# One decoder block on one core: the last two pairs' routing by straight logits, places written at once, and later deviations

## The chip, the cores and the metric

The kernel runs on one core of one Trainium2 chip. The metric is device time in microseconds, the median of three runs. One further execution was recorded by the hardware profiler; its trace gives the rows quoted here. Engines: PE is TensorE's matmul side (PEld its loading of weights), DVE VectorE, ACT ScalarE, POOL GpSimd, SP SyncE, which issues most of the DMAs. L1563 is line 1563 of the kernel before.

## The reference

One decoder layer over 16 sequences of 256 tokens of width 256, with a layer norm behind each of three residual parts. In the first attention the scores are `s / s`; the kernel forms that as a product of two such ratios, one of the queries and one of the keys, and weighs the values with its exps. The second is a differential cross attention: two softmaxes over the context, the second subtracted with a gain, each head then normalized. The third is a mixture of four experts with the two best chosen for each token:

```python
logits = jnp.einsum('bsh,he->bse', x, router_w) + router_b + load_balancer
rw, sel = jax.lax.top_k(logits, K)
rw = jax.nn.softmax(rw, axis=-1)
...
gathered = jnp.take_along_axis(stack, sel[..., None], axis=2)
return (rw[..., None] * gathered).sum(axis=2)
```

The change touches the end of the cross attention and the routing.

## The kernel before

**Tiles.** Two sequences make a pair (512 tokens, four chunks of 128); there are eight pairs, 0 to 7. The activations stay in SBUF in `xs`, tokens on partitions. Each expert gets only the tokens that chose it. For that every token's row is written by an indirect DMA, a "put" (L453), into a list in DRAM, at a place computed on the chip; there are two lists, one for pairs 0 to 6 and one for pair 7. A chunk has two puts, one for each chosen expert, so a pair has eight.

**Steps.** The cross attention runs as numbered steps. A step is a quarter of a unit (a pair, one of its sequences, four heads): score matmuls (`p`), the maximum on DVE, and three units later the scores again with exps on ACT (`e`), then the weighing `pob`. Other work is hung onto the steps by a small planner: `plan.at` and `later` run a function in a given step, `ahead` puts it first in its step, `job` queues it from a first step on with a due step. PE, DVE and ACT keep the order in which the code emits their instructions; POOL's and SP's orders in this stretch are chosen by the framework's scheduler from the dependences.

**The chain at the end of a pair.** `finish1` turns the weighed values back (pn, L1476), divides and subtracts (o on DVE, ob and the squares osq on POOL, L1485 and L1486). `finish2` makes the deviations of the heads: a sum on DVE (hv, L1493), then on POOL a reciprocal root by Newton steps and a product (L1494 to L1497). `finish4` turns the result (pto, L1506), `finish5` multiplies (pf) and adds (L1519), `norm` normalizes rows (POOL, up to L205). When both sequences are through, `turn_tokens` (pty, L1537) and the logits follow: `logits` holds the router's weights stationary, four chunks beside each other in 32 columns each; ACT copies the result (L1558), `turn_logits` turns it back on PE (ptl, L1563) and adds the bias on DVE. `routing` is a generator of five stages on DVE, POOL and ACT (selection, exp at L411, weights at L435). `places` counts with matmuls (pl), copies the lengths on DVE (L1581), and hands over to `listing`: rows (L442), then for each chunk the places on DVE (L451) and two puts. When a group's last pair is listed, POOL casts the counts (L463), waiting for all puts.

**The start of the experts.** `begin` loads the second expert's first two blocks of 512 rows from the list, every engine reads five counts (`known`, L500), and the first block is turned (pt, L527). The second expert's blocks (`early`) are mixed with the rest of pair 7: each is a turn of a later block, 16 matmul passes pw, 32 passes pr, and a store by SP (L556). Pair 7's finish, logits, routing and puts fall between these blocks.

`roomy(q)` is true for pairs 0 to 5. For pairs 6 and 7 nothing is spread over spare steps.

Of the kernel before, what the change touches and what calls it, by code (L numbers as in the profile page):

```python
# [15 lines left out]
P = 128  # L16
# [4 lines left out]
NPAIR = B // 2  # L21
TB = 2 * S
CPB = TB // P
# [77 lines left out]
def bc(ap, axis, n):  # L101

    shape = list(ap.shape)
    return ap.unsqueeze(axis).to_broadcast(shape[:axis] + [n] + shape[axis:])
# [3 lines left out]
def decoder_kernel(ctx: ExitStack, tc: tile.TileContext, a: dict, out: bass.AP):  # L108
# [46 lines left out]
    def mm(out_, lhsT, rhs, start=True, stop=True):  # L155
        PE.matmul(out=out_, lhsT=lhsT, rhs=rhs, start=start, stop=stop)  # L156
# [193 lines left out]
    moe, puts = {}, ([], [])  # L350

    def group(q):
        return int(q >= GROUPS[1][0])
# [35 lines left out]
    def routing(q, lg):  # L389

        ra = moe[q] = {}

        def tt(name, shape=(P, CPB, 4)):
            if name in ("gt", "eq", "sel", "mx"):
                return tiny.tile(list(shape), F32, tag=name, name=name)
            return moe["pool"].tile(list(shape), F32, tag=name, name=name, bufs=2 if name == "accs" else 1)

        gt, eq = tt("gt", (P, CPB, 4, 4)), tt("eq", (P, CPB, 4, 4))
        DVE.tensor_tensor(gt, bc(lg, 2, 4), bc(lg, 3, 4), ALU.is_gt)
        DVE.tensor_tensor(eq, bc(lg, 2, 4), bc(lg, 3, 4), ALU.is_equal)  # L400
        POOL.tensor_tensor(eq, eq, bc(moe["tri"], 1, CPB), ALU.mult)
        POOL.tensor_tensor(gt, gt, eq, ALU.add)
        yield
        larger, mx = tt("larger"), tt("mx", (P, CPB))
        DVE.tensor_reduce(larger, gt, AX.X, ALU.add)
        DVE.tensor_reduce(mx, lg, AX.X, ALU.max)
        sel = ra["sel"] = tt("sel")
        POOL.tensor_scalar(sel, larger, 2.0, None, ALU.is_lt)
        POOL.tensor_tensor(lg, lg, bc(mx, 2, 4), ALU.subtract)
        yield  # L410
        ACT.activation(lg, lg, AF.Exp)  # L411
        accs = ra["accs"] = tt("accs", (P, CPB + 1, 4))
        if q == GROUPS[group(q)][0]:
            POOL.memset(accs[:, 0], 0.0)
        else:
            POOL.tensor_copy(accs[:, 0], moe[q - 1]["accs"][:, CPB])
        for n in range(CPB):
            POOL.tensor_tensor(accs[:, n + 1], accs[:, n], sel[:, n], ALU.add)
        POOL.tensor_tensor(lg, lg, sel, ALU.mult)
        fore = tt("gt", (P, CPB, 4, 4))  # L420
        POOL.tensor_tensor(fore, bc(sel, 2, 4), bc(moe["tri"], 1, CPB), ALU.mult)
        yield
        den, nth = tt("mx", (P, CPB)), tt("nth")
        DVE.tensor_reduce(den, lg, AX.X, ALU.add)
        DVE.tensor_reduce(nth, fore, AX.X, ALU.add)
        DVE.reciprocal(den, den)
        both = ra["both"] = tt("both", (P, 2, CPB, 4))
        POOL.tensor_scalar(nth, nth, 1.0, None, ALU.is_lt)
        POOL.tensor_tensor(both[:, 0], sel, nth, ALU.mult)
        POOL.tensor_tensor(both[:, 1], sel, both[:, 0], ALU.subtract)  # L430
        POOL.tensor_tensor(lg, lg, bc(den, 2, 4), ALU.mult)
        w2 = tt("eq", (P, 2, CPB, 4))
        POOL.tensor_tensor(w2, both, bc(lg, 1, 2), ALU.mult)
        yield
        DVE.tensor_reduce(  # L435
            moe["weight"][:, q * CPB:(q + 1) * CPB, :].rearrange("p n k -> p k n"), w2, AX.X, ALU.add
        )
        yield
# [879 lines left out]
    def cross_attention(wb, r1, ps1):  # L1318
# [7 lines left out]
        for mp in mpads:  # L1326
# [5 lines left out]
        plan = Plan(  # L1332
            finish1=.55, turn_x=.55, turn_keys=.55, turn_tokens=.55, finish4=.55, project=1.05, values=1.9, finish5=1.9,
            logits=.6, turn_logits=.2, places=.6, weigh=1.85,
        )
# [3 lines left out]
        def apart():  # L1339
            return 1 if plan.now >= SINGLE else 2  # L1340
# [3 lines left out]
        cxs, xTs, es, ovs, oas, os_, sqs, ots = ({} for _ in range(8))  # L1344

        def bank(name):
            return banks[0].tile([P, 512], F32, tag="sm", name=name)
# [122 lines left out]
        def finish1(q, b, ic, t):  # L1470

            o = os_[q, b]
            pn = bank("pn")
            for k in range(4):
                i0 = t * S + ic * P
                PE.transpose(pn[:, k * P:(k + 1) * P], ovs[q, b, k][:, i0:i0 + P], ident)  # L1476
            pn_v = pn.rearrange("p (h d) -> p h d", h=H)
            rd = tiny.tile([P, H], F32, tag="rd", name="rdb")
            DVE.reciprocal(rd, pn_v[:, :, 16])
            if t == 1:  # L1480
                DVE.tensor_scalar(rd, rd, sec["gain"], None, ALU.mult)
            oas[t] = late[0].tile([P, H, HD], F32, tag="o2", name="o2", bufs=4)
            DVE.tensor_tensor(oas[t], pn_v[:, :, 0:16], bc(rd, 2, HD), ALU.mult)  # L1483
            if t == 1:
                POOL.tensor_tensor(o[:, ic], oas[0], oas[1], ALU.subtract)  # L1485
                POOL.tensor_tensor(sqs[q, b][:, ic], o[:, ic], o[:, ic], ALU.mult)  # L1486
                if ic == 1:
                    plan.later(4 if (q, b) <= (NPAIR - 2, 0) else 2, finish2, q, b)

        def finish2(q, b):  # L1490

# [36 lines left out]
        def roomy(q):  # L1528
            return q < NPAIR - 2

        def slack(q):
            return 3 if roomy(q) else 0
# [14 lines left out]

        def logits(q):

            pl = bank("pl")[:, :P]  # L1550
            for c in range(2):
                for n in range(CPB):
                    mm(
                        pl[32 * n:32 * n + 32, :], moe["rw"][:, c].rearrange("p a e -> p (a e)"),
                        xTs[q, c][:, n * P:(n + 1) * P], c == 0, c == 1,
                    )
            lT = moe["pool"].tile([P, P], F32, tag="lT", name="lT")
            ACT.copy(lT, pl)  # L1558
            plan.job(plan.now + apart(), plan.now + apart() + slack(q), turn_logits, q, lT)

        def turn_logits(q, lT):
            pt = bank("ptl")
            PE.transpose(pt[:, :P], lT, ident)  # L1563
            pl = pt[:, :P].rearrange("p (n a e) -> p n a e", n=CPB, e=4)[:, :, 0]
            lg = tiny.tile([P, CPB, 4], F32, tag="lg", name="lg")
            DVE.tensor_tensor(lg, pl, bc(moe["rb"], 1, CPB), ALU.add)
            route = routing(q, lg)
            for k in range(5):
                plan.ahead(1 + (2 * k if roomy(q) else k), next, route, None)
            wait = (FREE - 9 - plan.now) % 16 if roomy(q) else 0  # L1570
            plan.job(plan.now + 6 + wait, plan.now + 6 + wait + slack(q), places, q)

        def places(q):

            ra = moe[q]
            pb = bank("pl")
            pl = pb[:, :4 * CPB].rearrange("p (n e) -> p n e", e=4)
            if q + 1 == GROUPS[group(q)][1]:
                mm(pb[:, 4 * CPB:4 * CPB + 4], moe["ones"], ra["accs"][:, CPB])
                n = moe["length"]  # L1580
                DVE.tensor_copy(n[:, :4], pb[:, 4 * CPB:4 * CPB + 4])  # L1581
                DVE.tensor_tensor(n[:, 4:5], n[:, 0:1], n[:, 2:3], ALU.max)
            mm(pl, moe["before"], ra["sel"], True, False)
            mm(pl, moe["ones"], ra["accs"][:, :CPB], False, True)
            rows = moe["pool"].tile([P, CPB, 4], F32, tag="rows", name="rows")
            DVE.tensor_tensor(rows, pl, bc(moe["base"][:, group(q), :], 1, CPB), ALU.add)
            steps = listing(q, rows)
            plan.later(1, next, steps, None)
            plan.later(2, next, steps, None)
            for k in range(CPB):  # L1590
                if q < NPAIR - 3:
                    t = plan.now + 3 + (FREE - 3 - plan.now) % 16 + 4 * k
                else:
                    t = plan.now + (3 + 4 * k if q == NPAIR - 3 else 2 + k)
                plan.at(t, next, steps, None)
            plan.at(t + 1, next, steps, None)

# [151 lines left out]
```

## Time and profile before

| what | value |
| --- | --- |
| median of three runs | 1674.32 us (1673.7 to 1676.51) |
| profiled execution, device time | 1684.38 us |
| its span, first to last instruction | 1682.7 us, granted TensorE clock 0.983 |
| the cross attention's exps (L1435), first and last start | 605.7 and 1181.1 us |
| the first expert block's transposes begin | 1198.84 us |

The stretch that the change touches lies between about 1150 and 1290 us. The busy time of each engine in stages of it (from a table of windows; x is the number of instructions, then granted clock, DMA share and GB/s):

```profile
1170.00:1180.00 10.00, 8.43 (x61) 5.42 (x60) 1.40 (x10) 5.54 (x12) 6.50 (x28) 0.89 0.01 2
1180.00:1190.00 10.00, 8.37 (x44) 4.00 (x40) 3.01 (x10) 2.22 (x4) 5.85 (x7) 0.77 0.18 66
1190.00:1200.00 10.00, 1.16 (x6) 1.17 (x7) 0.00 (x0) 0.01 (x1) 3.34 (x5) 0.57 0.45 144
1200.00:1210.00 10.00, 10.00 (x36) 6.10 (x35) 3.19 (x9) 4.99 (x7) 4.08 (x16) 0.92 0.51 159
```

After the length of the window the columns are PE, PEld, DVE, ACT and POOL. PE is busy in nearly all of every window but the third, where it does 1.16 us in 10.

### The profile page before, as it was taken

The numbers are of one execution on the slowest core, as the hardware profiler recorded it, in microseconds if no ns is written. First come the engines' busy times: TensorE is split into PE (matmuls) and PEld (weight loads), VectorE is DVE, ScalarE is ACT, GpSimd is POOL, SyncE is SP. The second block draws the span as 40 slices with busy tenths as digits, with TensorE's granted clock in tenths as the row PEclk, the third lists the DMA queues.
The fourth block names the chain that finished last, engine by engine and source line by source line (L and its number), as shares of the span: only waits on it lengthen the run. The fifth ranks groups of instructions, "written<-read, shape, count | busy, mean of one in ns | idle before, by whom it ended". The sixth has DMA issues, their size and how long they took to land. (4 is left out here: it accounts for less than half of the span.)

```text
span 1682.7 us, 32337 instructions
## 1 busy us (share of the span) xinstructions
PE 1596.8 (95%) x12238; PEld 928.0 (55%) x12238; DVE 948.0 (56%) x1985; ACT 942.1 (56%) x1392; POOL 578.7 (34%) x1252
## 2 busy tenths in 40 slices
PE   7999999999999899999999999999799999899994
PEld 2333443444444466666666666665466566766673
DVE  2226656566666787777777777775213242323447
ACT  3557777888787856666666666666233211233212
POOL 5001243132123441243545535376331101046533
PEclk8999999999999999999999999999799999999997
DMA  9932121222222300000001000010326010132323
GB/s 251 302 106 70 64 72 64 74 67 67 98 65 76 115 15 2 16 2 15 28 20 35 15 16 21 9 40 27 102 86 220 1 51 14 54 113 64 95 65 126
DMA packets 118587, 115.34 MB, mean 69 GB/s; under 512 B 8208, under 2 KB 112352, under 8 KB 118400
## 3 DMA queue, kind: packets, MB, share of 16 engines
q1 hardware_dynamic: 109376, 93.08, 17.3%
q0 software_dynamic: 7824, 19.65, 3.8%
q8 instruction: 113, 1.85, 0.5%
q14 instruction: 74, 0.61, 0.1%
q10 hardware_dynamic: 1200, 0.15, 0.1%
HBM read 73.79 MB, written 38.54 MB: 67 GB/s over the span
## 5 line engine op out<-in xcount | busy, mean ns | idle before, releaser
L1429 DVE TENSOR_REDUCE mpad<-p 128x4 f32<-128x1024 f32 x256 | 303.3, 1217 | 114.2 <-PE p L156 109.3
L943 ACT ACTIVATE h<-ph,L_attn_b 128x1024 f32<-128x1024 f32 x256 | 271.2, 1111 | 140.8 <-PE ph L156 136.9
L1435 ACT ACTIVATE e<-p 128x512 f32<-128x512 f32 x512 | 269.7, 600 | 136.8 <-PE p L156 131.2
L156 PE MATMUL p<-qp,kT 32*128 32x256 f32 x2048 | 286.2, 393 | 4.4 <-issue 3.1
L156 PE MATMUL p<-kT,qp 32*128 32x256 f32 x2048 | 275.2, 392 | 3.9 <-DVE mpad L1429 3.8
L156 PEld LDWEIGHTS p<-kT,qp 32*128 32x128 f32 x2048 | 194.8, 184 | 50.3 <-issue 19.9
L156 PEld LDWEIGHTS p<-qp,kT 32*128 32x128 f32 x2048 | 206.9, 184 | 22.1 <-issue 8.1
L156 PE MATMUL ph<-qT,w1p 32*128 32x512 f32 x1024 | 163.7, 645 | 5.4 <-ACT h L943 4.2
L1044 DVE TENSOR_TENSOR z<-rqb,ra 128x1024 f32<-128x1024 f32 x120 | 151.5, 1268 | 3.1 <-DMA rqb<-rqd 3.1
L156 PE MATMUL pe<-h,w2p 128*32 128x512 f32 x1024 | 135.8, 600 | 0.0
L1051 ACT ACTIVATE z<-z 128x1024 f32<-128x1024 f32 x120 | 126.6, 1057 | 0.3 <-DVE z L1044 0.3
L156 PE MATMUL pob<-e,vaug 128*32 128x512 f32 x1024 | 124.6, 605 | 0.1
L156 PEld LDWEIGHTS ph<-qT,w1p 32*128 32x128 f32 x1024 | 47.6, 184 | 123.9 <-ACT h L943 88.6
L201 POOL TENSOR_SCALAR ln_ve<-ln_mv 128x2 f32<-128x2 f32 x32 | 8.8, 276 | 247.9 <-DVE ln_mv L199 246.8
L205 POOL TENSOR_SCALAR xs<-xs,ln_mv,rs_y 128x256 f32<-128x256 f32 x64 | 85.5, 1341 | 2.8
L156 PE MATMUL pw<-xeT,L_ffn_sw_w 128*128 128x512 f32 (+1 forms) x256 | 83.3, 486 | 1.9 <-PEq L734 1.9
L156 PE MATMUL po<-z,vaug 128*32 128x256 f32 x1024 | 73.2, 385 | 5.7 <-ACT z L1051 3.6
L453 POOL DMA_INDIRECT xlist<-xs,place x64 | 64.0, 1000 | 35.2 <-DVE place L451 13.2
L156 PEld LDWEIGHTS pw<-xeT,L_ffn_sw_w 128*128 128x128 f32 x256 | 48.6, 190 | 35.3 <-issue 31.0
L1485 POOL TENSOR_TENSOR ob<-o,o 128x256 f32<-128x256 f32 x32 | 23.5, 735 | 124.4 <-DVE o L1483 111.9
L156 PE MATMUL pw<-xeT,L_ffn_ml_w 128*128 128x512 f32 (+1 forms) x160 | 63.3, 552 | 0.3 <-DVE ye L555 0.3
L528 ACT ACT_TABLE_LOAD x16 | 20.5, 1283 | 76.6 <-PE pt L527 76.3
(378 smaller groups left out, 2582.2 us busy)
## 6 DMA issues: line engine op xcount, KB each, us to landing
rqb<-rqd SPq DMA_DIRECT2D x64, 512.0 KB
xlist<-zero SPq DMA_DIRECT2D x16, 1024.0 KB
xe<-xlist SPq DMA_DIRECT2D x20, 512.0 KB
xlist<-ye SPq DMA_DIRECT2D x14, 512.0 KB
xs<-in_x SPq DMA_DIRECT2D x8, 512.0 KB
cx<-in_ctx SPq DMA_DIRECT2D x8, 512.0 KB
qp<-st SPq DMA_DIRECT2D x256, 2.0 KB
out<-xs SPq DMA_DIRECT2D x7, 512.0 KB
```

Of the source, the lines that this page charges most:

```text
L156: PE.matmul(out=out_, lhsT=lhsT, rhs=rhs, start=start, stop=stop)
L201: POOL.tensor_scalar(ve, mv[:, :, 1], EPS, None, ALU.add)
L205: POOL.tensor_scalar(x, x, mv[:, i, 0:1], r[:, i:i + 1], ALU.subtract, ALU.mult)
L453: put = POOL.indirect_dma_start(xlist[g][:], bass.IndirectOffsetOnAxis(ap=place[:, n, k:k + 1], axis=0), xs[:, q * CPB + n, :], None)
L528: copies[c](t[:, c, :n * P], pt[:, :n * P])
L943: ACT.activation(h, phs[gp], AF.Tanh, bias=b1[:, fc:fc + 1])
L1044: DVE.tensor_tensor(z, bc(rqbs[u][:, 2 * gp:2 * gp + 2], 2, 2), bc(rk, 3, S), ALU.mult)
L1051: ACT.activation(z, z, AF.Exp)
L1429: DVE.tensor_reduce(mpads[j % 2][:, 2 * gp:2 * gp + 2, :, ic], p1, AX.X, ALU.max, negate=True)
L1435: ACT.activation(e[:, gi], p2[gi], AF.Exp)
L1485: POOL.tensor_tensor(o[:, ic], oas[0], oas[1], ALU.subtract)
```

## The change

Three edits, none of which changes what is computed:

1. The puts of pairs 6 and 7: all four chunks' places and puts are emitted in the same step, two steps after `places`; before, chunk k came k steps later.
2. The deviations (`finish2`) of pair 7's first sequence come eight steps after `finish1` in place of two, and those of its second sequence four in place of two. All others keep theirs.
3. The logits of pairs 6 and 7: each chunk's tokens are the stationary operand and the router's four columns the moving one, so that the result has tokens on partitions at once. The copy on ACT and the transposition on PE go, and the routing starts in the step of the logits, one step earlier. Pairs 0 to 5 keep the old way; the tail of `turn_logits` becomes the function `route`.

```diff
                 if ic == 1:
-                    plan.later(4 if (q, b) <= (NPAIR - 2, 0) else 2, finish2, q, b)
+                    plan.later({(NPAIR - 2, 1): 2, (NPAIR - 1, 0): 8}.get((q, b), 4), finish2, q, b)
...
         def logits(q):
 
+            if not roomy(q):
+                pl = bank("pl")[:, :4 * CPB].rearrange("p (n e) -> p n e", e=4)
+                for n in range(CPB):
+                    for c in range(2):
+                        mm(pl[:, n, :], xTs[q, c][:, n * P:(n + 1) * P], moe["rw"][:, c, 0], c == 0, c == 1)
+                return route(q, pl)
             pl = bank("pl")[:, :P]
...
             PE.transpose(pt[:, :P], lT, ident)
-            pl = pt[:, :P].rearrange("p (n a e) -> p n a e", n=CPB, e=4)[:, :, 0]
+            route(q, pt[:, :P].rearrange("p (n a e) -> p n a e", n=CPB, e=4)[:, :, 0])
+
+        def route(q, pl):
             lg = tiny.tile([P, CPB, 4], F32, tag="lg", name="lg")
             DVE.tensor_tensor(lg, pl, bc(moe["rb"], 1, CPB), ALU.add)
-            route = routing(q, lg)
+            stages = routing(q, lg)
             for k in range(5):
-                plan.ahead(1 + (2 * k if roomy(q) else k), next, route, None)
+                plan.ahead(1 + (2 * k if roomy(q) else k), next, stages, None)
...
-                    t = plan.now + (3 + 4 * k if q == NPAIR - 3 else 2 + k)
+                    t = plan.now + (3 + 4 * k if q == NPAIR - 3 else 2)
```

In the instruction order of the changed kernel, against the one before: PE's place matmuls of pair 6 stand two score quarters earlier; pair 7's first pto stands between the transposes of the first two expert blocks, where one pn stood, and its pf behind the first block's product; on POOL the eight puts of pair 6 stand together, behind them the chain L1494 to L1497 of pair 7's first sequence, then the cast of the counts; on SP the load of the fifth block stands behind the first store.

## The prediction

> **What bounds the kernel now.** I read the busy row and the slices first, then PE's waits between 1100 and 1320 us, where every instruction that the diff touches runs, then the timelines of PE, POOL, ACT and DVE there.
>
> ```profile
> PE 1596.8 (95%) x12238; PEld 928.0 (55%) x12238; DVE 948.0 (56%) x1985; ACT 942.1 (56%) x1392; POOL 578.7 (34%) x1252
> ```
>
> TensorE is busy almost throughout, so a change in this stretch pays only where PE stands still. Its waits there (who waited for whom: us in total, times, longest) begin with
>
> ```profile
> PE pt L527 <- DMA xe<-xlist: 9.8, 1, 9.8
> PE pt L527 <- issue: 2.5, 1, 2.5
> PE pl L156 <- DVE length L1581: 2.3, 2, 1.6
> ```
>
> One long wait: the transposes of the first expert block, for rows loaded from the list in DRAM. PE's timeline (columns: start, us, engine, line, tiles, count, idle time before) shows its ends, POOL's what it hangs on:
>
> ```profile
> 1187.19 1.89 PE L156 MATMUL pf<-L_xattn_woT,otb 128*128 128x256 f32 x8
> 1198.84 1.97 PE L527 MATMUL pt<-ident,xe 128*128 128x128 f32 x8 [9.76 <-DMA xe<-xlist]
> ```
>
> ```profile
> 1179.80 1.07 POOL L453 DMA_INDIRECT xlist<-xs,place  x1 [0.70 <-DVE place L451]
> ...
> 1187.59 0.96 POOL L453 DMA_INDIRECT xlist<-xs,place  x1 [2.92 <-DVE rdb L1479]
> ...
> 1192.52 0.99 POOL L453 DMA_INDIRECT xlist<-xs,place  x1 [0.17 <-issue]
> 1195.20 0.18 POOL L463 CAST count<-length 128x5 int32<-128x5 f32 x1 [1.69 <-DMA xlist<-xs,place]
> ```
>
> The eight puts of pair 6 (L453) complete the list. The last ends at 1193.51, the queue issues the load 1.45 us later, at 1194.96, and the rows are there 3.88 us after that. Beside it runs a second path: the cast of the counts (L463), then every engine reads five counts (L500; PE's first starts at 1195.4, the last at 1197.3 for 0.31), so PE could have gone on at 1197.6. The rows were later, by 1.2 us. Behind 1198.84 PE is dense for the 90 us in which the second expert runs, so what moves PE's restart, or adds PE work behind it, moves the end.
>
> **Part 1: when the list is complete.** Pair 6's logits begin at 1162.05 on PE. Now 8 matmuls, packed four abreast in 32 columns, take 0.57 us (next instruction 1162.62), ACT copies the result, PE transposes it at 1167.35 (0.26 to the next start). After the change each of the 8 has 128 tokens as weights and four moving columns. The before trace has no such logits; it has the same shape at the bias products (128x128 weights, one moving column, two passes a matmul):
>
> ```profile
> 113.96 0.60 PE L156 MATMUL pb<-L_ffn_me_eq_b,m 128*128 128x1 f32 x4
> 114.42 0.58 PE L156 MATMUL pb<-L_ffn_me_bv,m 128*128 128x1 f32 x4
> 114.87 0.58 PE L156 MATMUL pb<-L_ffn_me_bo,L_ffn_me_c1w 128*128 128x1 f32 x4
> ```
>
> Starts 0.455 apart for four passes: 0.112 us a pass, 16 passes 1.80 us. Here a rule is to be weighed. The Trainium skill, "TensorE: Matmul & The Clock Gate", section Back-to-back issue gap, gives a matmul of 1 to 64 moving columns about 25 ns: 16 passes would be 0.40 us (an estimate from that page). The same page's section on LDWEIGHTS says that loading goes by weight columns, 128/1.2 = 107 ns. The row says that the weights set the pace here, so I take 1.80; with 0.40 the whole sum below would be about 1.4 us better at pair 6 and 1.4 at pair 7, -3.4 in place of -0.6. From the other side, the plain transposes go at 0.148 a pass (four in 0.59): 2.4 us each time.
>
> So PE is 1.80 - 0.57 - 0.26 = 0.97 later at the score quarter that now starts at 1167.61. From there ACT's exps set the pace (they run unbroken from 1168.77 to 1171.81), and the exp of the logits (L411) slips between them for 0.11 (now 1171.64 to 1171.75). The weighing pob of 1171.94 starts at 1173.02 and takes 1.86: the places' matmuls start at 1174.88, now 1175.70, because two quarters (1.90 us) that stand ahead of them are behind them in the new order.
>
> Now they stall there: the first starts at 1175.70, the second at 1177.62, since DVE copies the lengths (L1581) only after the weights (L435), which wait for POOL's routing, which is interleaved with pair 7's deviations (L1494 to L1497, 1169.17 to 1175.46). With the deviations moved behind the puts, and the logits on DVE at 1164.1 in place of 1167.71, I follow the routing row by row to the weights at about 1173.2, before PE comes; 0.60 (0.36 and the copy) are left. Second matmul: 1175.48. From it to the first put takes 2.18 as now (1177.62 to 1179.80): 1177.66.
>
> Puts: four now wait 2.92 us for their places on DVE, behind reciprocals that wait for PE, and let ob and osq in between: 13.71 us from 1179.80 to 1193.51. With all places written at once they run as pair 7's eight do now, 1269.22 to 1279.17, 9.95 us. **Last put: 1187.6, 5.9 us earlier.**
>
> **Part 2: what is late next.** The moved deviations come back. In the instruction order of the changed kernel POOL has, between the last put and the cast, the whole chain L1494 to L1497 of pair 7. Undisturbed it takes 5.52 us (1129.90 to 1135.42). The rows land at 1187.6 + 1.45 + 3.88 = 1192.9. The cast, which could run at 1189.3, ends at 1187.6 + 0.1 + 5.52 + 0.18 = 1193.4, and PE reads five counts for 2.23 us more: **PE restarts at 1195.6**, not 1198.84, a gain of 3.2. The wait changes hands from the DMA to the counts, and 2.7 of the 5.9 stay behind.
>
> **Part 3: PE work moved over the gap.** Now PE does pair 7's first pto and pf (L1506 at 1180.49, pf at 1187.19) ahead of its wait, for nothing. In the new order the fourth pn goes ahead, the pto takes its place between the first blocks' transposes (0.59 for 0.59), and the pf stands behind the first block's product: +1.83 us (the other pf, 1232.14 to 1233.97), on the path.
>
> What waits for it: DVE's residual (L1519), the deviations of (7,1) (hv L1493 is behind it in DVE's order) and POOL's two chains, which are interleaved. hv comes about 3.4 us after the first block's end, and 7.5 us of POOL end 10.9 after it; the pto that needs them comes after 1.83 + 0.87 + 13.9 = 16.6. Cover 5.7 us, so nothing. The load of block 4 moves behind the first store on SP: needed 34 us later, nothing.
>
> **Part 4: pair 7's logits,** on the path too. Now the first half starts at 1249.95 beside ACT's second copy, and the next transposes at 1251.67. In the new order the first matmul waits for both copies, 1250.69, and 1.80 us follow: 1252.49, **+0.82**. ACT's lT copy and the transposition are in the 1251.67 already. Pair 7's places come 14 us later, behind the block's product, and its puts stand together now: nothing from that edit.
>
> **Sum:** -3.2 + 1.83 + 0.82 = -0.55. The profiled execution (span 1682.7 of 1684.38) should read about 1682.1; on the median of the runs, 1674.32, the same microseconds give **1673.7**. A second rule bears on the gap: the same page, part 1, lets PE run at half clock after an idle window of about 3.4 us, until a busy one. The granted clock was 0.60 from 1198.8 to 1202.4, and the 20 transposes there took 3.60 us against 2.33 at the warm pace: 1.27 lost, by the rule 1.7. PE's work before the gap ends near 1185, so 10 us of idle time remain and neither is won back.
>
> **Rivals.**
> - Counts in time (0.12): the cast or the reading of the counts costs less than I take, and PE restarts with the rows, at 1192.9: -5.9 + 2.65 = -3.3, 1671.0, or more if the logits are cheaper too. For it: the reading is hidden in the trace, and POOL's chain has short steps. Against it: the order is fixed, the chain stands before the cast.
> - Puts that throttle each other (0.11): two puts of pair 5 at 1162.98 and 1165.31 stood 2.33 us apart with nothing shown between, not 1.27. If four of the eight pay that 1.06, the last put ends at 1191.8, PE restarts at 1199.8, and the sum is +1.0 + 2.65 = +3.6: 1677.9. It decides from a mean spacing of about 1.8 us. Against it: pair 7's eight, back to back at 1.28.
> - Dear logits (0.07, no change in the end): 2.4 us each, +0.6 twice: +0.6, 1674.9.
> - The early places don't come early, because the routing is late for PE as now (0.05): 2.1 of the 5.9 are lost, +1.6, 1675.9.
>
> **How the numbers follow.** Forecast 0.65, 1673.7, its own range 1671.8 to 1675.6 (5.0 to 5.8 for the chain, 1.7 to 2.4 for the logits, 1 us for places on ACT's pace). A measurement of this kernel can tell about 0.2%, 3.3 us, from no change. The forecast, dear logits and late places lie within it (0.77, of which I give 0.02 to the edge): same 0.75. Faster has its rival and a little of that edge, 0.13; slower has the puts' rival and the rest, 0.12. The range that leaves 2 in 10 out is 1670.6 to 1677.4.
>
> **What would show it.** Right: the last L453 of pair 6 near 1187.6 and without waits among the eight; L463 some 5.7 us behind it, released by POOL's own chain; the first pt<-xe at 1195 to 1196, waiting for counts and no more for the DMA; a pf of 1.8 us behind the first block's pr; pl at pair 7 as 16 passes of 0.11. Wrong: puts further apart than 1.3 us, pl matmuls that stall for DVE again, or a wait of pto for POOL in the second expert's blocks.

## The result and the profile after

| kernel | median | runs |
| --- | --- | --- |
| before | 1675.74 us | 1673.7 to 1676.51, 6 runs |
| changed | 1682.4 us | 1678.56 to 1684.91, 6 runs |

The changed kernel is slower: ratio 1.0036, 95% interval 1.0023 to 1.0049, or some 6 us, where 0.6 us less was forecast. (The three runs of before given above are among the six here.) In two later comparisons it gave 1.0014 (1.0004 to 1.0025) and 1.0035 (1.0022 to 1.0048).

PE's waits in the stretch, in the same view as before (who waited for whom: us in total, times, longest):

```profile
PE pt L527 <- POOL ob L1485: 8.8, 1, 8.8
PE pt L527 <- issue: 2.5, 1, 2.5
...
PE pl L156 <- DVE length L1589: 1.0, 2, 0.8
```

The long wait has changed hands as forecast: the rows (DMA) no longer end it. The name ob is that of the last POOL instruction that the trace could tie to it; what PE waited for is the count, as POOL's timeline shows (start, us, engine, line, tiles, count, idle before):

```profile
1179.78 1.07 POOL L453 DMA_INDIRECT xlist<-xs,place  x1 [0.70 <-DVE place L451]
...
1188.74 0.96 POOL L453 DMA_INDIRECT xlist<-xs,place  x1 [0.30 <-issue]
1189.77 0.22 POOL L1494 TENSOR_SCALAR hv<-hv 128x32 f32<-128x32 f32 x1
1194.22 1.06 POOL L1497 TENSOR_TENSOR ob<-ob,rs_y 128x512 f32<-128x512 f32 x1
1195.22 0.19 POOL L463 CAST count<-length 128x5 int32<-128x5 f32 x1
```

Eight puts in 9.92 us, none waiting, then the moved chain, then the cast. But the first put is late, and PE's timeline shows why:

```profile
1159.47 1.95 PE L156 MATMUL pl<-rw,x 128*128 128x4 f32 x16
1161.34 1.13 PE L156 MATMUL p<-qp,kT 32*128 32x256 f32 x8
...
1162.99 2.09 PE L156 MATMUL p<-qp,kT 32*128 32x256 f32 x8
1165.01 3.64 PE L156 MATMUL pob<-e,vaug 128*32 128x512 f32 x16
...
1177.28 0.39 PE L156 MATMUL pl<-accs,ones 128*128 128x4 f32 x2
1177.91 0.40 PE L156 MATMUL pl<-sel,before 128*128 128x16 f32 x2 [0.26 <-DVE length L1589]
```

The logits take 1.87 us from start to start. The eight score matmuls behind them take 1.13 us, the next eight 2.09, and the weighing pob 3.64. In the profile of before the same stretch reads

```profile
1162.05 0.65 PE L156 MATMUL pl<-x,rw 128*32 128x128 f32 x16
...
1164.35 1.21 PE L156 MATMUL p<-qp,kT 32*128 32x256 f32 x8
1165.49 1.92 PE L156 MATMUL pob<-e,vaug 128*32 128x512 f32 x16
```

So PE of the changed kernel runs at about half speed from 1163 on. In windows of 2 us (length, PE, PEld, DVE, ACT, POOL, then granted clock, DMA share, GB/s):

```profile
1160.00:1162.00 2.00, 2.00 (x19) 1.93 (x20) 0.51 (x3) 0.56 (x2) 1.23 (x2) 1.00 0.04 14
1162.00:1164.00 2.00, 2.00 (x15) 1.50 (x13) 0.85 (x4) 1.08 (x2) 1.26 (x2) 0.83 0.15 51
1164.00:1166.00 2.00, 2.00 (x13) 0.69 (x14) 0.41 (x3) 1.09 (x2) 1.92 (x6) 0.50 0.18 66
1166.00:1168.00 2.00, 2.00 (x16) 0.26 (x8) 0.00 (x0) 0.00 (x0) 1.07 (x6) 0.50 0.00 0
1168.00:1170.00 2.00, 2.00 (x15) 1.35 (x15) 0.00 (x0) 0.58 (x1) 0.00 (x0) 0.50 0.00 0
```

PE counts as busy 2.00 us of every 2.00, and its clock falls to 0.50 all the same. In the profiled execution of before the clock was 1.00 up to 1177, for instance

```profile
1164.00:1166.00 2.00, 2.00 (x20) 1.20 (x22) 0.92 (x3) 1.30 (x3) 0.69 (x1) 1.00 0.18 66
```

Executions differ in when they reach this stretch (the start of pair 6's logits, t0, lay between 1159.4 and 1163.5 us), so traces are compared from t0. All marks in us behind it; "pair 7 through" is the first transposes behind pair 7's logits, "end" the transposes ahead of pr<-xw (1293.09 in the profile of before):

| kernel | first places' matmul | first put | last put ends | cast ends | PE restarts | pair 7 through | end |
| --- | --- | --- | --- | --- | --- | --- | --- |
| before, profile shown | 13.65 | 17.75 | 31.46 | 33.33 | 36.79 | 89.62 | 131.04 |
| before, second trace | 15.29 | 17.76 | 29.68 | 31.55 | 35.17 | 89.50 | 130.92 |
| forecast | 12.83 | 15.61 | 25.55 | 31.35 | 33.55 | 89.07 | |
| changed, profile | 17.81 | 20.31 | 30.23 | 35.94 | 38.16 | 93.52 | 135.02 |
| changed, second trace | 15.95 | 18.46 | 28.38 | 34.09 | 36.34 | 91.82 | 133.30 |
| changed, third trace | 16.00 | 18.50 | 28.43 | 34.14 | 36.37 | 92.58 | 135.52 |

When pair 7 is through the changed kernel is 2.2 to 4.0 us behind before, at the end of the stretch 2.3 to 4.6.

### The profile page after: what moved, and what is told of

It reads as the page before. It is cut to its first block, busy times and chain, and to the rows that moved or that the text cites. A ratio compares the mean times of both kernels' runs of the same rounds, so it can differ in the third digit from the quotient of the medians.

```text
span 1676.9 us, 32328 instructions
## 1 busy us (share of the span) xinstructions
PE 1596.9 (95%) x12236; PEld 927.8 (55%) x12236; DVE 945.5 (56%) x1985; ACT 941.4 (56%) x1390; POOL 579.7 (35%) x1252
## 3 DMA queue, kind: packets, MB, share of 16 engines
q8 instruction: 112, 1.84, 0.4%
## 5 line engine op out<-in xcount | busy, mean ns | idle before, releaser
L156 PE MATMUL pob<-e,vaug 128*32 128x512 f32 x1024 | 129.6, 626 | 0.1
L1462 ACT COPY ovTb<-pob 128x512 f32<-128x512 f32 x64 | 37.5, 585 | 61.7 <-PE pob L156 61.7
```

The source lines that it names most:

```text
L1462: ACT.copy(o, po)
```

## The experiments

Kernels of one group ran on the same chip, beside the kernel before.

**First group: the parts alone.** Theory: the straight logits bring PE's clock down and eat the gain. Rival: the moved work (POOL's chain ahead of the counts, pf behind the gap) costs more than reckoned.

*before_again* is the kernel before, unedited.

> The kernel before, unchanged, for a second trace of it. Expected ratio 1.000. In the trace: 36.8 us from the start of pair 6's logits to the first transposes of the first expert block (xe), and a granted clock of 1.00 in the 10 us after those logits. If the half clock seen there in the changed kernel is chance and not its logits, it may show up here too.

Measured: 0.9998 (0.9989 to 1.0007). The clock is 1.00 for 10.3 us behind t0, then 0.50 for 3.4 us. The restart comes 1.6 us earlier than in the profile shown, yet pair 7 is through at the same time: the clock stays at half for 13.7 us around the gap in place of 10.2.

*packed_both* takes the changed kernel and gives pairs 6 and 7 their packed logits back:

```diff
-            if not roomy(q):
+            if q >= NPAIR:
```

> The changed kernel with both packed logits and the transposition back in place: places at once and deviations later alone. Theory 'half clock' (the eight straight logits, N=4, bring the granted clock down for the 7 us behind them, which ate the gain): clock 1.00 in the 10 us after the logits, 33 to 35 us from the logits to the first xe transposes (before 36.8, changed 37.8), ratio to before between 0.9988 and 1.0005. Rival 'exposed work' (the loss comes from POOL's chain ahead of the counts and the pf moved behind the gap): still 37 us or more to the xe transposes and a ratio near 1.003.

Measured: 1.0053 (1.0039 to 1.0066). The clock did stay at 1.00 for 10 us, and the kernel is slower still: both theories missed. Its trace has the chain between the puts (11.17 us from the first to the last put's end), and at pair 7 PE stands 2.46 us for the lengths, where before stood 0.76.

*straight_only* is the third edit on the kernel before, that is, the changed kernel with the other two undone:

```diff
-                    plan.later({(NPAIR - 2, 1): 2, (NPAIR - 1, 0): 8}.get((q, b), 4), finish2, q, b)
+                    plan.later(4 if (q, b) <= (NPAIR - 2, 0) else 2, finish2, q, b)
...
-                    t = plan.now + (3 + 4 * k if q == NPAIR - 3 else 2)
+                    t = plan.now + (3 + 4 * k if q == NPAIR - 3 else 2 + k)
```

> The kernel before with the straight logits of pairs 6 and 7 alone. Theory 'half clock': clock near 0.5 for some 6 us after pair 6's logits, 3 us more than before up to the xe transposes (some 39 to 40 us) and 0.8 at pair 7: ratio 1.002 to 1.003. Rival 'price of the matmuls only': clock 1.00 there, 37.8 us or less to the xe transposes, since the logits reach DVE 3 us earlier; ratio 1.0000 to 1.0010.

Measured: 1.002 (1.0011 to 1.0028). Half clock for 10.2 us from 1 us behind t0 on; first put at 20.06 in place of 17.76. The eight puts then stand together (9.93 us) with no edit 1. Whether that is because the clock has delayed them until all places are ready, or because the routing starts a step earlier, was not tested. The restart was not 39 to 40 us behind t0, but 35.4.

*places_only* is the first edit on the kernel before:

```diff
-                    t = plan.now + (3 + 4 * k if q == NPAIR - 3 else 2 + k)
+                    t = plan.now + (3 + 4 * k if q == NPAIR - 3 else 2)
```

> The kernel before with the four places of pair 6 at once, and nothing else of the change: pf and the deviations of the last pair stay ahead of the gap, the logits are packed. The eight puts in 9.95 us without waits, the cast right behind them, the first xe transposes by the rows again, 33.1 us after the logits (before 36.8): 3.7 us gained, ratio 0.998. If the puts aren't what sets the restart: 36 us or more and a ratio of 1.000.

Measured: 0.9989 (0.998 to 0.9998), its restart at 32.85 as expected, pair 7 through 2.4 to 2.5 us earlier than in the two traces of before.

**Second group: the deviations, and the clock held by work.** *dev_only* is the second edit alone on the kernel before:

```diff
-                    plan.later(4 if (q, b) <= (NPAIR - 2, 0) else 2, finish2, q, b)
+                    plan.later({(NPAIR - 2, 1): 2, (NPAIR - 1, 0): 8}.get((q, b), 4), finish2, q, b)
```

> The kernel before with the deviations of the last pair later and nothing else. Theory 'deviations are the dear part': pf behind the gap (+1.8), POOL's chain between the puts or ahead of the cast, at pair 7 the counts of the list late by some 1.7 us as with both logits packed (2.46 us of wait for the lengths there against 0.76): ratio 1.003 to 1.006. Rival 'only the mixture is bad': ratio within 1.0000 to 1.0015.

Measured: 1.0067 (1.0054 to 1.008), the slowest of all. Its POOL timeline shows two places:

```profile
1184.84 1.06 POOL L1497 TENSOR_TENSOR ob<-ob,rs_y 128x512 f32<-128x512 f32 x1
1186.05 0.99 POOL L453 DMA_INDIRECT xlist<-xs,place  x1 [0.15 <-issue]
...
1268.55 0.26 POOL L428 TENSOR_SCALAR nth<-nth 128x16 f32<-128x16 f32 x1 [12.28 <-DVE mx L426]
```

The scheduler sets the chain among the puts, which take 15.2 us. At pair 7 POOL's routing waits 12.28 us for DVE, whose order has a copy of the expert block (L528) ahead of the routing's next stage (L424):

```profile
1254.56 0.68 DVE L528 COPY xeT<-pt 128x512 f32<-128x512 f32 x1
1268.16 0.17 DVE L424 TENSOR_REDUCE mx<-lg 128x4 f32<-128x16 f32 x1
```

PE waits 2.46 us for the lengths there and half clock follows for 6.8 us. In the changed kernel, with straight logits, DVE finishes the routing first and PE waits 0.78 us; so there the third edit mends part of what the second does. In one mixture further down (after_seven_one) it does not.

*places_straight* is the first and third edit without the second:

```diff
-                    plan.later({(NPAIR - 2, 1): 2, (NPAIR - 1, 0): 8}.get((q, b), 4), finish2, q, b)
+                    plan.later(4 if (q, b) <= (NPAIR - 2, 0) else 2, finish2, q, b)
```

> The changed kernel with the deviations (finish2) at their old times: places at once and straight logits alone. If the deviations later cost nothing but are part of the gain: ratio 1.0036 or more. If they cost the pf behind the gap and POOL's chain ahead of the counts (the other theory), this comes out near straight_only, 1.0015 to 1.0025: pf ahead of the gap, xe transposes some 35 us after the logits and waiting for the rows, since the straight logits alone already let the eight puts stand together.

Measured: 1.0005 (0.9997 to 1.0013), below the expectation and below straight_only's 1.002, which was taken on another chip: the later deviations are no part of a gain.

*after_fill* sets dense work among pair 6's straight logits:

```diff
-                pl = bank("pl")[:, :4 * CPB].rearrange("p (n e) -> p n e", e=4)
+                pb = bank("pl")
+                pl = pb[:, :4 * CPB].rearrange("p (n e) -> p n e", e=4)
                 for n in range(CPB):
                     for c in range(2):
                         mm(pl[:, n, :], xTs[q, c][:, n * P:(n + 1) * P], moe["rw"][:, c, 0], c == 0, c == 1)
+                    for c in range(2 if q == NPAIR - 2 else 0):
+                        mm(pb[:, 256:512], xTs[q, c][:, n * P:(n + 1) * P], xTs[q, c][:, :256])
```

> The changed kernel with eight dense matmuls (128x128 weights, 256 moving columns) set between pair 6's straight logits; their results are not read. They cost 1.7 us of PE. Theory 'half clock' (a window of thin work brings the clock down, dense work holds it): granted clock 1.00 in most of the 7 us behind the logits instead of 0.50, the first put 16.5 to 18 us after the start of the logits (changed 19.96) in spite of the added work, ratio to before 1.0015 to 1.003, under the changed kernel's 1.0036. Rival 'matmul price and moved work': the clock has nothing to do with it; the first put comes 1.7 us later still (21 to 22 us) and the ratio is 1.0045.

Measured: the clock stays at 1.00 for 28 us behind t0, and the first put comes at 18.96 although the added work takes 3.6 us (5.44 us for the block, 1.87 without): a matmul of 256 fp32 columns is two passes of 0.22 us, twice what the expectation took. Ratio 1.0045 (1.0032 to 1.0058), the one that the rival named: the clock moved as the theory said, the time did not. The filler costs as much as the held clock saves up to the first put (18.46 to 20.31 in the traces without it).

*places_warm* is places_only with 24 such matmuls behind the pf ahead of the gap, results not read:

```diff
+            if (q, b) == (NPAIR - 1, 0):
+                pz = bank("pz")
+                for i in range(24):
+                    mm(pz[:, :256], ots[b][:, 0, 0, :], sec["woT"][:, 0, :])
```

> The kernel before with the places at once, and 24 dense matmuls (5.2 us at full clock, results not read) on PE behind the pf ahead of the gap. Theory 'the gap's cold clock costs': PE stands still for 3 us instead of 8, the granted clock from the restart on is 1.00 instead of 0.50 for 6 us, and some 2 to 3 us more are gained: ratio 0.9970 to 0.9980 (places at once alone 0.9989). Rival 'clock falls anyway, or the filler delays the counts': 0.9985 to 0.9995.

Measured: 1.002 (1.0011 to 1.0028). The filler ran 10.5 us and over the restart (35.15). Its trace has full clock from there until pair 7 is through, at 86.56, no later than places_only. By the ratios it is some 5 us above that kernel all the same, and its trace has these 5 us far behind the stretch. A block of a later expert starts level (439.34 us behind t0, 439.74 in places_only); then PE waits for ACT:

```profile
1604.00 15.24 PE L156 MATMUL pw<-xeT,L_ffn_sw_w 128*128 128x256 f32 x60 [2.68 <-ACT hid L580]
```

The clock is at half for 6.8 us there, and the block's 64 passes take 18.86 us in place of 13.89. Why ACT is late, and whether it is so in every execution, one trace doesn't show.

**Third group: the second edit in two.** *after_again* is the changed kernel, unedited.

> The changed kernel, unchanged, for a second trace of it. Expected ratio 1.003 to 1.0045. In the trace: half clock in some 7 of the 10 us behind pair 6's logits, 37 to 39 us from the logits to the first xe transposes, which wait for the counts; pf behind the first block. Open: why its median is some 3 us above what the first trace explains. If half clock behind pair 7's logits is the rest, a window of 0.50 stands behind 1250 us in this trace, as it does in two of the four other traces with straight logits there.

Measured: 1.0014 (1.0004 to 1.0025), below the expectation, its marks in the table; no half clock behind pair 7's logits. On this chip before itself has a median of 1682.04 us.

*after_seven_zero* and *after_seven_one* undo half of the second edit each; (7,0) and (7,1) are pair 7's first and second sequence. First the one, then the other, each against the changed kernel:

```diff
-                    plan.later({(NPAIR - 2, 1): 2, (NPAIR - 1, 0): 8}.get((q, b), 4), finish2, q, b)
+                    plan.later({(NPAIR - 2, 1): 2, (NPAIR - 1, 0): 8, (NPAIR - 1, 1): 2}.get((q, b), 4), finish2, q, b)
```

```diff
-                    plan.later({(NPAIR - 2, 1): 2, (NPAIR - 1, 0): 8}.get((q, b), 4), finish2, q, b)
+                    plan.later({(NPAIR - 2, 1): 2, (NPAIR - 1, 0): 2}.get((q, b), 4), finish2, q, b)
```

> The changed kernel with only the second half of the later deviations undone: those of (7,1) after 2 steps as before, those of (7,0) after 8. Theory '(7,0) is the dear one' (POOL's chain between last put and cast, pf behind the gap): ratio as the changed kernel, 1.0025 to 1.0045. Rival '(7,1) pushes pair 7's routing back': near places_straight, 1.0000 to 1.0012.

> The changed kernel with only the first half of the later deviations undone: those of (7,0) after 2 steps as before, those of (7,1) after 4. Theory '(7,0) is the dear one': pf ahead of the gap, the chain ahead of the puts, xe transposes some 36 us after the logits and waiting for the rows; ratio 1.0000 to 1.0012. Rival '(7,1)': 1.0025 to 1.0045.

Measured: 1.0031 (1.002 to 1.0042) both. The first has the marks of after_again to 0.1 us at every column, so (7,1) costs the changed kernel nothing that a trace shows in this stretch; why its ratio is 0.0017 above that of after_again, these marks don't show. The second missed its expectation: with (7,0) back, the wait of 2.44 us for pair 7's lengths appears as in dev_only, and half clock stands for 10.2 us behind pair 6's logits. The two halves are not independent; the split fails as a way to share out the loss.

*places_warm12* is the same with `range(11)`.

> Places at once with 11 dense matmuls behind the pf in place of 24: one of these takes 0.43 us and not the 0.22 that was taken for places_warm, whose filler so ran 10.5 us and over the restart. 4.7 us of filler, PE idle for some 3.3 us, restart by the rows 32.9 us after the logits as in places_only, at a granted clock of 1.00 from 1 us behind it at the latest. Theory 'the gap's cold clock costs': ratio 0.9970 to 0.9985. Rival 'no gain': 0.9985 to 1.0005.

Measured: 0.9972 (0.9961 to 0.9982). But this is the chip on which the changed kernel gave 1.0014, and its trace has the restart at 32.80 at half clock for 6.8 us, as without filler, and the end at 128.48, where places_only has 128.58. That the filler gives anything is not shown.

**Fourth group: the shares, on one chip.** *after_third* is the changed kernel, *places_straight2* and *places_only2* are the kernels above, *after_fill4* is after_fill with half the fillers:

```diff
-                    for c in range(2 if q == NPAIR - 2 else 0):
+                    for c in range(1 if q == NPAIR - 2 else 0):
```

> The changed kernel, unchanged, on the chip that runs the three kernels below. It gave 1.0036 and 1.0014 on two chips; expected between them, 1.0014 to 1.0036.

> Places at once and straight logits, deviations at their old times, on the same chip as the changed kernel. Theory 'the later deviations carry the loss': 0.0015 to 0.003 under the changed kernel's ratio, 1.0000 to 1.0012. Rival 'the straight logits carry it': within 0.001 of the changed kernel.

> Places at once alone, on the same chip. If the straight logits' half clock costs what its traces show (accs 4 us later, 3 us at the third expert): 0.001 to 0.002 under places_straight2, that is 0.998 to 0.9995.

> The changed kernel with four dense matmuls (128x128 weights, 256 columns, results not read) between pair 6's straight logits in place of the eight of after_fill, 1.75 us of PE work. Theory 'half clock': the granted clock stays 1.00 in the 10 us behind t0 and the first put comes 17 to 17.5 us after the start of the logits (changed 18.5 to 20.3), ratio no higher than the changed kernel's. Rival 'four aren't enough': half clock for 3.4 or 6.8 us again, first put at 20 to 22 us.

| kernel | ratio to before | restart | pair 7 through | end |
| --- | --- | --- | --- | --- |
| places_only2 | 0.9991 (0.9983 to 0.9999) | 32.75 | 86.65 | 128.07 |
| places_straight2 | 1.0011 (1.0004 to 1.0017) | 33.75 | 87.62 | 130.54 |
| after_third | 1.0035 (1.0022 to 1.0048) | 36.37 | 92.58 | 135.52 |
| after_fill4 | 1.0017 (1.0009 to 1.0025) | 35.10 | 91.78 | 135.00 |

All four came within what was expected of them. So places at once gain 0.0009 (1.5 us); the straight logits then cost 0.0020 (3.3 us), the later deviations another 0.0024 (4.0 us), each uncertain by about 0.001 (the last by 0.0015), reckoned from the intervals. The last step's place is plain, because the list is complete at the same time in both kernels (last put 28.39 and 28.43). Without the chain behind it, in places_straight2, POOL and PE read:

```profile
1187.69 0.96 POOL L453 DMA_INDIRECT xlist<-xs,place  x1 [0.30 <-DMA xlist<-xs,place]
1190.35 0.19 POOL L463 CAST count<-length 128x5 int32<-128x5 f32 x1 [1.70 <-DMA xlist<-xs,place]
```

```profile
1185.03 1.89 PE L156 MATMUL pf<-L_xattn_woT,otb 128*128 128x256 f32 x8
1194.01 1.97 PE L527 MATMUL pt<-ident,xe 128*128 128x128 f32 x8 [7.08 <-DMA xe<-xlist]
```

The cast comes 1.70 us behind the last put and PE restarts with the rows, 5.36 us behind it; with the chain there, by the counts, 7.94 us behind it: 2.6 us. The pf stands ahead of the gap here and behind it in the changed kernel: 1.9 more.

And after_fill4 does 1.8 us more work than the changed kernel and is 3.0 us faster by the ratios (medians 1679.04 and 1682.35 us; the two intervals just overlap). Its windows and the start of its places:

```profile
1161.00:1163.00 2.00, 2.00 (x16) 1.90 (x16) 0.00 (x0) 0.00 (x0) 0.72 (x1) 1.00 0.18 66
1163.00:1165.00 2.00, 2.00 (x15) 1.27 (x14) 0.53 (x3) 0.34 (x1) 1.60 (x3) 1.00 0.18 66
1165.00:1167.00 2.00, 2.00 (x19) 1.18 (x20) 1.11 (x5) 1.38 (x4) 0.68 (x1) 1.00 0.00 0
```

```profile
1166.37 1.92 PE L156 MATMUL pob<-e,vaug 128*32 128x512 f32 x16
...
1174.51 0.39 PE L156 MATMUL pl<-accs,ones 128*128 128x4 f32 x2
1175.15 0.40 PE L156 MATMUL pl<-sel,before 128*128 128x16 f32 x2 [0.25 <-DVE length L1592]
```

PE is as busy as in the changed kernel's windows and keeps its full clock; pob takes 1.92, not 3.64. So the half clock comes of how thin the work is, and not of PE standing still as the profile counts it: both kernels with filler kept their clock. Which property of the thin work counts, the few moving columns or the many weight loads, was not separated. Where the 3.0 us are won is not shown either: pair 7 is through 0.8 us earlier than in after_third and level with after_again (91.82), with the clock at half for 13.7 us around the restart, in place of 10.2 and 6.8.

## Why the prediction was wrong

**The step that failed** is in part 1, the way from the logits to the puts: "From there ACT's exps set the pace", "the places' matmuls start at 1174.88", and so "first put ... 1177.66". It counted every PE instruction there at its full-clock duration, and so put the clock at nothing. The three traces of the change have the first put 18.46 to 20.31 us behind t0, not 15.61. With the clock held, after_fill4 and after_fill have it at 17.22 and 18.96; less their filler (1.84 and 3.57) both give 15.4, and 33.3 for the restart that was forecast at 33.55. So the instruction counts were right to 0.3 us and the clock was the missing term: 2.9 to 4.7 us. All eight traces with unfilled straight logits have the clock at half within 1 to 4 us of t0, for 6.8 or 10.2 us; of the eight with packed logits none has before 10 us.

Even with the clock held the forecast gain would not have come. Pair 7 is through at 91.78 and 93.10 in these two kernels, less their filler 89.9 and 89.5 (an estimate from these traces), and before has 89.62 and 89.50: half clock for 13.7 us around the gap takes what was won at the restart.

The second rule weighed was the one that bears on this, and it was applied to the gap alone. The Trainium skill, "TensorE: Matmul & The Clock Gate", part 1 (The HAM clock gate), has half clock follow an idle window of about 3.4 us. No idle window stands here, so that rule, as worded, would not have warned; the traces agree with its length (every stretch at half clock in this part of the kernel is 3.4, 6.8, 10.2, 13.7 or 17.1 us) and go beyond it in what counts as idle.

**Right, term by term.** The logits: 1.87 us against 1.80 (starts 0.455 apart for four passes are 0.114 a pass, not 0.112, and 1.82 in all), so they go at the pace of the bias products, as it took them, and not at 0.40. The puts: 9.92 to 9.93 against 9.95. The chain and cast behind them: 5.71 against 5.8. The reading of the counts: 2.22 to 2.25 against 2.23. From the restart until pair 7 is through: 55.36, 55.48 and 56.21 us against 52.83 + 1.83 + 0.82 = 55.48. The 0.82 is right in its sum and not in its split: pair 7's first logits do not wait for the second copy, but its 16 passes wait 0.41 us for it between them. The wait of pto for POOL did not appear.

**By edits.** The second edit was reckoned at 2.7 (the gain that stays behind the chain) and 1.83 (pf), 4.5 us; by the ratios of the fourth group it costs 4.0, by the marks at the end of the stretch 3.3 to 5.0. The first and third together were to gain 5.1 us; by their two ratios they lost 0.8 and 1.8. The miss of 6 to 7 us is there. The clock has 2.9 us of it (first put 18.48 in places_straight2, against 15.61) to 4.7 (20.32 in places_straight). Another 1.8 is the starting point: the profile shown has the last put at 31.46, the second trace at 29.68, with half clock for 6.8 us and for 3.4 us while the puts ran, and both are through pair 7 at the same time. So a late last put in one execution was reckoned as something to gain. In places_straight these two cover the miss; in places_straight2 2.2 us are left, for which the half clock behind pair 7's straight logits, worth 1.7 us there, is a candidate that was not tested.

**The rivals.** Counts in time: no, the cast ended 5.7 us behind the last put. Puts that throttle: no, they stand 1.26 to 1.38 us apart. Dear logits: no. Places late: by name yes, but not by its cause; the lengths kept PE waiting 0.26 us, and it was PE itself that came late. The slower outcome had its chance in a rival whose mechanism did not occur.

**Open.** The traces put the change 2.3 to 4.6 us behind at the end of the stretch; the three ratios say 2.3 to 6. Half clock for 3.4 us behind pair 7's logits stands in one of three traces of the change (five of ten with straight logits there) and would be 1.7 us each time; more executions than were traced would be needed to say if that is the rest. Behind the stretch single executions differ by more than the change: before needs 389.6 us from the end mark to its end in one trace and 382.8 in the other. So the totals are read from the medians and ratios, and the traces only for where the time goes in the stretch.

**A version that beats both** is places_only: 0.9989 and 0.9991 on two chips, both intervals below 1.

## What to carry to other kernels

Before costing work on PE at its durations, look at the granted clock around it, and ask whether the new instructions are thin: here many weight loads with few moving columns slowed what stood behind them. When a step is moved later, the same engine's next duty (here the cast that frees every engine) pays for it, and a change of one due time can push another step behind a block in a different engine's order; so each part of a change is worth a run alone. Reckon gains on marks that two executions of the kernel before agree on.

## What was unexpected of the hardware

- PE busy 2.00 us in 2.00, yet granted 0.50: sixteen passes of 128x128 weights with four columns, 1.9 us among 32-row score matmuls, were enough to bring the clock down for 6.8 to 10.2 us. Four dense matmuls among them, 1.84 us in all, held it at 1.00.
- In this part of the kernel half clock came in multiples of 3.4 us, each worth up to 1.7 us of work, and not in every execution: behind pair 7's straight logits it stands in five of ten traces. An earlier restart behind the gap may be followed by a longer stretch at half clock: before's two traces restart 1.6 us apart and are level 54 us later.
- It can fall without such logits, among score matmuls of 32 rows: in before_again and packed_both the clock fell for 3.4 us some 10.3 us behind t0, with no wait of PE over 0.17 us since t0.
